# A two-layer mixture-of-experts block: the two-sided decayed sum as a scan of a scan, with its clamps on GpSimd, and another order in layer 0's routed tiles

## Chip, cores and metric

One core of one Trainium2 chip runs the whole program. The metric is the device time of one execution in microseconds (us); a time stands for the median of several runs. A profile is one execution seen by the hardware profiler: engines are PE (TensorE, matrix products), PEld (its weight loads), DVE (VectorE), ACT (ScalarE), POOL (GpSimd) and SP (SyncE, which issues DMAs).

## The reference, cut to what matters

There are two layers. Each has a "cond" step that mixes a side input k (4 x 512 x 512) along time, and a feed-forward step with routed experts plus a shared expert. All in float32. With T = 512 time steps and C = 512 channels, for each batch b and channel c:

```
tf    = sigmoid(sum(time_emb))
decay = exp(-exp(w)) * (0.5 + 0.5*tf)            # one number per (b, c), below 1
ek    = exp(min(k, 30));  ekv = ek * v           # v is k here
a[t]  = a[t-1]*decay + e[t]                      # scan forward  -> nf (of ekv), df (of ek)
a[t]  = a[t+1]*decay + e[t]                      # scan backward -> nb, db
euk   = exp(min(u + k, 30))
num   = nf + nb - ekv + euk*v;  den = df + db - ek + euk
out   = sigmoid(x) * num / max(den, 1e-8) * (0.8 + 0.2*tf)
```

So each of num and den is a two-sided sum, over all s, of decay^|t-s| e[s], plus one more term. Layer 0's feed-forward is: RMS norm, softmax over 8 experts, the top 2, SiLU-gated experts of width 256, and a shared expert of width 256. Layer 1's: softmax over 32 experts, the top 6, experts of width 352, a shared expert of width 704. Each layer adds its result to x.

## The kernel before

**Layer 0's loop of units.** A unit is one batch b (of 4) and one block c of 128 channels (of 4): 16 units, channels on the partitions and 512 time steps along the free axis. The order on ACT, PE and DVE is the program's own (a manual schedule); POOL and SP are ordered by the tile framework's planner. Iteration n of the loop does, in this order: `sums(n-1)`, `front(n+1)`, `front_exps(n+1)`, `turn(n+3)`, then routing and shared-expert pieces of the batch before, `mid(n)`, and `back(n-1)`.

- `turn` transposes k's rows on PE into `kA`. The rows of one batch lie in the tile `kr`, of which there is one; `load_k(b+1)` is asked for on SP once the last unit of batch b has been turned, together with `load_x(b+1)`.
- `front` (L401 to L409) does the two clamps on DVE (`ek` L406, `euk` L408), `front_exps` the exponentials on ACT (L414).
- `mid` multiplies with k on DVE (`ekv` L425, `eukv` L426) and calls `scans` (L258): for ek and for ekv one scan forward over 512 steps (L263) and one backward over 511 steps that leaves the own element out (L264), each into a tile of its own. Four scans a unit.
- `sums` adds the three parts on PE into PSUM, with an identity as the weight: `den` = df + dx + euk, `num` = -(nf + nx + eukv) times the batch's factor: six matrix products a unit (L436 to L438). ACT makes a reciprocal from den (`r`, L440 to L442).
- `back` (L449 to L452) makes num/den and multiplies it onto the sigmoids in `zT`.

Between units lie layer 0's router (`route_*`), whose slots are written one indirect DMA per (tile, choice) from POOL into `table0` (`fill_table`, L353), and the shared expert for some tiles (`share_*`). At the start POOL also writes the blank tables (L248 to L250) and 16 blocks of zeros to the DRAM tensor `xb` (L254).

**Layer 0's routed tiles.** `routed(0, ...)` runs expert after expert, in tiles of 128 rows, the first unconditionally, the others under nested `tc.If(n > s*P)` (L892). `slot_tile` puts on PE: gate products (L835), the transposes of the hidden rows of the tile before (`turn_hidden`, L799), up products (L839), the transposes of the next tile's rows (`turn_rows` into `pza`, L785), and the down products of the tile before (`put_out` into `pout`, L813). On ACT: SiLU (`sgt`, L842), the copy of the hidden rows of the tile before (`hT`, L804), the scaled up result (`upt`, L845), four scaled copies of the transposed rows (`zgT`, L789), the copy of `pout` to `ob` (L815) and of `last` (L862). On POOL: the product `hrow` (L846), the gather of the tile after the next (L772, an indirect DMA), and the scatter-add of the tile before (L818). In layer 0 the gate's and the up's results share one PSUM bank (`pgu`), and `pout` has one bank: three banks (`late`) are held for the shared expert's last three tiles.

Beside the routed tiles DVE does layer 1's two-sided sums (`wkv1`: 16 units, L915 to L925, into `kA`). They are needed when layer 1 begins. Then come the last three shared tiles, layer 1's input with its router (L965 to L986), layer 1's shared expert with the router's slots (L1060 to L1072), and layer 1's routed tiles.

Of the kernel before, what the change touches and what calls it, by code (L numbers as in the profile page):

```python
# [25 lines left out]
DEN_MIN = 1e-8  # L26
EXP_LN = "natural_log_exp_and_others"
# [3 lines left out]
def adaln_ffn_kernel(  # L31
# [90 lines left out]
    def load_k(b):  # L122
        kr = wk.tile([P, TB, D], F32, tag="kr", name=f"kr{b}", bufs=1)
        nc.sync.dma_start(kr, kf[b * S : (b + 1) * S, :].rearrange("(i p) c -> p i c", p=P))
        return kr
# [54 lines left out]
    kr = wk.tile([P, TB, D], F32, tag="kr", name="kr0", bufs=1)  # L180
    for i in range(TB):
        nc.scalar.dma_start(kr[:, i, :], kf[i * P : (i + 1) * P, :])
    load_x(0)
    gaten = acc[:E1, NT - 3, :]
# [9 lines left out]
            engines={mybir.EngineType.Activation, mybir.EngineType.PE, mybir.EngineType.DVE}  # L194
# [20 lines left out]
    for l in range(2):  # L215
        ew = const.tile([P, NC], F32, name=f"ew{l}")
        nc.scalar.activation(ew, wch[l], AF.Exp)
        dw = const.tile([P, NC], F32, name=f"dw{l}")
        nc.scalar.activation(dw, ew, AF.Exp, scale=-1.0)
        dec = const.tile([P, NC, B], F32, name=f"dec{l}")  # L220
        nc.vector.tensor_tensor(
            dec, dw.unsqueeze(2).to_broadcast([P, NC, B]), half.unsqueeze(1).to_broadcast([P, NC, B]), ALU.mult
        )
        decay.append(dec)
# [20 lines left out]
    for tb, width in ((table0, 3), (table1, 2)):  # L245
        blank = wk.tile([P, NCOL * width], F32, name=f"blank{width}", tag="lgT", bufs=1)
        bv = blank.rearrange("p (c w) -> p c w", w=width)
        nc.gpsimd.memset(bv, 0.0)  # L248
        nc.gpsimd.memset(bv[:, :, 0], EMPTY)
        nc.gpsimd.dma_start(tb.rearrange("(p c) w -> p (c w)", p=P), blank)  # L250
    zero = wk.tile([P, D], F32, name="zero", tag="zr", bufs=TB)
    nc.gpsimd.memset(zero, 0.0)
    for t in range(NT):
        nc.gpsimd.dma_start(xb[t * P : (t + 1) * P, :], zero)  # L254


    L = S - 1

    def scans(l, b, c, ek, ekv, df, dx, nf, nx):

        dec = decay[l][:, c, b : b + 1]
        for v, f, r in ((ek, df, dx), (ekv, nf, nx)):
            nc.vector.tensor_tensor_scan(f, dec.to_broadcast([P, S]), v, 0.0, ALU.mult, ALU.add)  # L263
            nc.vector.tensor_tensor_scan(  # L264
                r[:, L - 1 :: -1],
                v[:, L:0:-1],
                dec.to_broadcast([P, L]),
                0.0,
                ALU.add,
                ALU.mult,  # L270
            )

# [113 lines left out]
    def turn(n):  # L386

        nonlocal kr
        if n >= NU:
            return  # L390
        b, c = units[n]
        pk = bank("tr", f"pk{n}")
        for i in range(TB):
            nc.tensor.transpose(pk[:, i * P : (i + 1) * P], kr[:, i, c * P : (c + 1) * P], ident)
        nc.scalar.copy(kA[:, c, b * S : (b + 1) * S], pk)
        if c == NC - 1 and b + 1 < NB:
            kr = load_k(b + 1)
            load_x(b + 1)

    def front(n):  # L400
# [4 lines left out]
        ek = wk.tile([P, S], F32, tag="ek", name=f"ek{n}", bufs=2)  # L405
        nc.vector.tensor_scalar(ek, kT, 30.0, None, ALU.min)  # L406
        euk = wk.tile([P, S], F32, tag="euk", name=f"euk{n}", bufs=3)
        nc.vector.tensor_scalar(euk, kT, uch[0][:, c : c + 1], 30.0, ALU.add, ALU.min)  # L408
        fronts[n] = ek, euk  # L409

    def front_exps(n):
        if n < NU:
            for v in fronts[n]:
                nc.scalar.activation(v, v, AF.Exp)  # L414

    def mid(n):
        b, c = units[n]
        kT = kA[:, c, b * S : (b + 1) * S]
        ek, euk = fronts.pop(n)

        def tmp(tag, bufs=2):
            return wk.tile([P, S], F32, tag=tag, name=f"{tag}{n}", bufs=bufs)

        ekv, eukv = tmp("ekv", 1), tmp("eukv")
        nc.vector.tensor_tensor(ekv, ek, kT, ALU.mult)  # L425
        nc.vector.tensor_tensor(eukv, euk, kT, ALU.mult)  # L426
        df, dx, nf, nx = tmp("df"), tmp("dx"), tmp("nf"), tmp("nx")
        scans(0, b, c, ek, ekv, df, dx, nf, nx)
        mids[n] = (df, dx, euk), (nf, nx, eukv)

    def sums(n):
# [3 lines left out]
        for p, m, (f, r, o) in zip((den, num), (ident, nfac[:, b, :]), mids.pop(n)):  # L435
            nc.tensor.matmul(p, m, f, start=True, stop=False)  # L436
            nc.tensor.matmul(p[:, :L], m, r[:, :L], start=False, stop=False)
# [124 lines left out]
    def route_slots(b):  # L562
# [4 lines left out]
        through(fill_table(table0, sloti, pay, TB, 2, "table0" if b == NB - 1 else None))  # L567
# [53 lines left out]
    def exps1_upto(m):  # L621
        nonlocal done
        while done < m:
# [3 lines left out]
            nc.scalar.activation(ek, kT, AF.Exp)  # L627
# [13 lines left out]
    for n in range(NU + 1):  # L641
        b, c = divmod(n, NC)
        if n:
            sums(n - 1)
        front(n + 1)
# [29 lines left out]
        if c == 3 and b >= 1:  # L675
            route_slots(b - 1)
        if c == 2 and b >= 1:
# [34 lines left out]
    route_slots(NB - 1)  # L712
    counts0 = const.tile([P, E0], I32, name="counts0")
# [26 lines left out]
    def routed(l, pool, px, E, NS, chunks, zd, tab, put_at, counts, outs, first_weights, load, then=None, extra={}):  # L740
# [3 lines left out]
        if l == 0:  # L744
            pgu = px.tile([P, 2 * F], F32, name="pgu0")
            pg, pu = pgu[:, :F], pgu[:, F:]
        else:
            pg = px.tile([P, F], F32, name="pgate1")
            pu = px.tile([P, F], F32, name="pup1")
        pout = [px.tile([P, D], F32, name=f"pout{l}{h}") for h in range(1 + l)]  # L750
# [77 lines left out]
        def slot_tile(e, s, wts, due):  # L828

            gv, uv, _ = wts  # L830
            zt = turned(e, s)
            if due is not None and l == 1:
# [19 lines left out]
            gather(e, s + 2)  # L852
# [46 lines left out]
        return ahead, pza, phT  # L899

    latep = ExitStack()
    late_ps = latep.enter_context(tc.tile_pool(name="late", bufs=1, space=PSUM))
    late_out = [late_ps.tile([P, D], F32, name=f"late{t}") for t in range(LATE, NT)]
    with tc.tile_pool(name="r0", bufs=1) as rp, tc.tile_pool(name="px0", bufs=1, space=PSUM) as px:
# [5 lines left out]
        def wkv1(n):  # L910
# [3 lines left out]
            ekv, df, dx, nf, nx = [rp.tile([P, S], F32, tag=f"v{i}", name=f"v{i}_{n}") for i in range(5)]  # L914
            nc.vector.tensor_scalar(ek, ek, E30, None, ALU.min)  # L915
            nc.vector.tensor_tensor(ekv, ek, kT, ALU.mult)
            scans(1, b, c, ek, ekv, df, dx, nf, nx)
            nc.vector.tensor_tensor(df[:, :L], df[:, :L], dx[:, :L], ALU.add)
            nc.vector.tensor_tensor(nf[:, :L], nf[:, :L], nx[:, :L], ALU.add)
            nc.vector.scalar_tensor_tensor(df, euk, E30, df, ALU.min, ALU.add)  # L920
            nc.vector.scalar_tensor_tensor(ekv, euk, E30, kT, ALU.min, ALU.mult)
            nc.vector.tensor_tensor(nf, nf, ekv, ALU.add)
            nc.vector.tensor_scalar(df, df, DEN_MIN, None, ALU.max)
            nc.vector.reciprocal(df, df)
            nc.vector.scalar_tensor_tensor(kT, nf, fac[:, b : b + 1], df, ALU.mult, ALU.mult)  # L925
# [13 lines left out]
        with tc.manual_schedule(engines={mybir.EngineType.Pool, mybir.EngineType.PE, mybir.EngineType.Activation}):  # L939
            (wnext,), pza, phT = routed(  # L940
# [5 lines left out]
            for t in range(LATE, NT):  # L946
# [3 lines left out]
                if t > LATE:  # L950
                    share_turn(t - 1, phT)
                    share_down(t - 1, po=late_out[t - 1 - LATE])
            share_turn(NT - 1, phT)
            share_down(NT - 1, po=late_out[NT - 1 - LATE])
# [38 lines left out]
    latep.close()  # L993
# [120 lines left out]
```

## Time and profile before

| | |
|---|---|
| median of 3 runs | 1601.48 us (1598.72 to 1601.71) |
| the profiled execution: its time, its span | 1601.9 us, 1600.1 us |
| PE busy | 1458.0 us (91%) |
| DVE busy | 678.1 us (42%) |
| POOL busy | 593.0 us (37%) |
| ACT busy | 399.9 us (25%) |

The stages, read from the timeline: start to 44 us the first loads and the first three units; to about 205 us the rest of layer 0's loop; to 262 us the last router batch and shared tiles; to 557 us layer 0's routed tiles; to 626 us the late shared tiles and layer 1's input; the rest is layer 1. A number in front of a timeline row is the start in us from the span's beginning, the next the duration; what stands in brackets is the idle time of that engine ahead of it and what ended it. "issue" is time in which the engine waited for nothing that the profile shows.

### The profile page before, as it was taken

What the parts mean: (1) busy time and instruction counts of PE and PEld (TensorE: products, weight loads), DVE (VectorE), ACT (ScalarE), POOL (GpSimd) and SP (SyncE); (2) the same over time, 40 slices, a digit from 0 to 9 for tenths busy, and PEclk for the clock granted to TensorE, in tenths of its full rate; (3) what the DMA queues carried; (4) which work ended last, traced back from release to release, by engine and by line L of the source; (5) the groups of instructions that cost most, each with busy time, mean ns of one, the idle gap of its engine ahead of it and who ended that gap; (6) DMA issues with size and microseconds to landing.
All of it is one profiled execution on the core that took longest, in us unless ns stands there. A gap on an engine that the chain in (4) does not pass through costs nothing. (4 is left out here: it accounts for less than half of the span.)

```text
span 1600.1 us, 16354 instructions
## 1 busy us (share of the span) xinstructions
PE 1458.0 (91%) x5097; PEld 860.8 (54%) x5097; DVE 678.1 (42%) x1192; ACT 399.9 (25%) x966; POOL 593.0 (37%) x576
## 2 busy tenths in 40 slices
PE   4878988979788788999999999999999999999997
PEld 2445555656555466444444565555555555655654
DVE  6897956999960035261111222222222222222221
ACT  4755534454333324000000111111111111111110
POOL 3020133767654300016663333344333443433332
PEclk8999999999989879999999999999999999999999
DMA  9210114444545364001113655565645585565542
GB/s 351 80 33 34 40 47 163 73 100 77 111 109 125 86 223 153 1 1 43 39 46 109 181 150 130 145 191 153 164 109 136 128 266 119 130 187 131 122 99 40
DMA packets 117177, 184.95 MB, mean 116 GB/s; under 512 B 19928, under 2 KB 65004, under 8 KB 117016
## 3 DMA queue, kind: packets, MB, share of 16 engines
q1 hardware_dynamic: 80120, 122.14, 22.6%
q0 software_dynamic: 36336, 60.04, 19.8%
q8 instruction: 66, 1.08, 0.3%
q10 hardware_dynamic: 576, 1.05, 0.2%
q14 instruction: 79, 0.65, 0.1%
HBM read 152.07 MB, written 52.64 MB: 128 GB/s over the span
## 5 line engine op out<-in xcount | busy, mean ns | idle before, releaser
L813 PE MATMUL pout<-w,hT 128*128 128x512 f32 (+1 forms) x432 | 206.9, 612 | 10.6 <-ACT hT L804 9.3
L818 POOL DMA_INDIRECT out_dram<-ob,put x52 | 82.6, 1589 | 282.7 <-DVE ob L817 142.2
L772 POOL DMA_INDIRECT acc<-z1d,put x119 | 123.3, 1036 | 136.7 <-PE pza L785 58.9
L353 POOL DMA_INDIRECT table<-pay,r1sloti x96 | 93.3, 972 | 195.1 <-DVE hid L1063 168.6
L851 DVE SCALAR_TENSOR_TENSOR hrow<-pup,tab,sgt 128x352 f32<-128x352 f32 x84 | 49.1, 584 | 257.6 <-issue 131.2
L835 PE MATMUL pgate<-w,zgT 128*128 128x352 f32 x416 | 133.2, 463 | 0.1
L839 PE MATMUL pup<-w,zgT 128*128 128x352 f32 x416 | 131.5, 459 | 0.0
L817 DVE COPY ob<-pout 128x512 f32<-128x512 f32 x84 | 58.1, 692 | 172.7 <-PE pout L813 166.8
L813 PEld LDWEIGHTS pout<-w,hT 128*128 128x128 f32 (+1 forms) x432 | 77.8, 194 | 83.8 <-issue 55.7
L785 PE MATMUL pza<-ident,acc 128*128 128x128 f32 x584 | 88.8, 277 | 21.3 <-DMA acc<-z0d,put 18.1
L785 PEld LDWEIGHTS pza<-ident,acc 128*128 128x128 f32 x584 | 71.7, 142 | 65.3 <-issue 27.5
L353 POOL DMA_INDIRECT table<-r0pay,r0sloti x32 | 36.0, 1125 | 182.9 <-DVE r0sloti L343 137.4
L839 PEld LDWEIGHTS pup<-w,zgT 128*128 128x128 f32 x416 | 79.0, 190 | 44.0
L835 PEld LDWEIGHTS pgate<-w,zgT 128*128 128x128 f32 x416 | 75.8, 192 | 34.0 <-issue 1.2
L808 ACT COPY hT<-phT 96x128 f32<-96x128 f32 x84 | 22.0, 262 | 285.3 <-DVE hT L806 285.3
L1060 PE MATMUL g<-zT,w 128*128 128x512 f32 (+1 forms) x192 | 89.3, 609 | 4.2 <-DVE lg L991 4.2
L795 ACT COPY zgT<-pza 128x256 f32<-128x256 f32 x103 | 38.3, 373 | 210.3 <-DVE zgT L794 158.7
L813 PE MATMUL pout<-zT,hT 128*128 128x512 f32 (+1 forms) x192 | 87.8, 593 | 0.0
L1060 PE MATMUL u<-zT,w 128*128 128x512 f32 (+1 forms) x192 | 86.3, 592 | 0.0
L1069 PE MATMUL o<-w,hid 128*128 128x512 f32 (+1 forms) x192 | 83.8, 592 | 0.0
L835 PE MATMUL pgate<-zT,zgT 128*128 128x352 f32 x256 | 81.0, 459 | 0.0
L839 PE MATMUL pup<-zT,zgT 128*128 128x352 f32 x256 | 81.0, 459 | 0.0
(279 smaller groups left out, 2346.9 us busy)
## 6 DMA issues: line engine op xcount, KB each, us to landing
w<-in_L_ffn_w_dram SPq DMA_DIRECT2D x44, 704.0 KB, 5.9
zT<-in_L_ffn_w_dram SPq DMA_DIRECT2D x20, 704.0 KB, 5.0
w<-in_L_ffn_w_dram SPq DMA_DIRECT2D x22, 512.0 KB
zT<-in_L_ffn_w_dram SPq DMA_DIRECT2D x10, 512.0 KB
w<-in_L_ffn_w_dram SPq DMA_DIRECT2D x22, 192.0 KB, 8.9
xb<-zero POOLq DMA_DIRECT2D x16, 256.0 KB, 7.8
acc<-in_x_dram SPq DMA_DIRECT2D x4, 1024.0 KB, 15.2
z0d<-zr SPq DMA_DIRECT2D x16, 256.0 KB, 2.0
```

The lines of the kernel that those rows point to most:

```text
L353: ins = nc.gpsimd.indirect_dma_start(out=table, out_offset=bass.IndirectOffsetOnAxis(ap=sloti[:, t, j : j + 1], axis=0), in_=pay[:, t, j, ...
L772: nc.gpsimd.indirect_dma_start(out=rows(e, s), out_offset=None, in_=zd, in_offset=bass.IndirectOffsetOnAxis(ap=put_at[:, e * NS + s : e * ...
L785: nc.tensor.transpose(pza[which][:, c * P : (c + 1) * P], rows(e, s)[:, c * P : (c + 1) * P], ident)
L795: nc.scalar.copy(dst[:, h:, :], pza[which][:, h * P :].rearrange("p (c t) -> p c t", c=h))
L813: nc.tensor.matmul(po, hT[:m, j, :], dv[:m, j, :], start=(j == 0), stop=(j == nf - 1))
L817: nc.vector.tensor_copy(row, po)
L818: nc.gpsimd.indirect_dma_start(out=outs[n % len(outs)], out_offset=bass.IndirectOffsetOnAxis(ap=at, axis=0), in_=row, in_offset=None, boun ...
L835: nc.tensor.matmul(pg, zt[:, c, :], gv[:, c, :], start=(c == 0), stop=(c == NC - 1))
L839: nc.tensor.matmul(pu, zt[:, c, :], uv[:, c, :], start=(c == 0), stop=(c == NC - 1))
L851: nc.vector.scalar_tensor_tensor(hrow, pu, tab[:, col, 1:2], sgt, ALU.mult, ALU.mult)
L1060: nc.tensor.matmul(p[:m], wv[:, c, f : f + m], zT[:, c, cols], start=(c == 0), stop=(c == NC - 1))
L1069: nc.tensor.matmul(po, hid[:m, j, i * P : (i + 1) * P], dv[:m, j, :], start=(j == 0), stop=(j == len(FCH) - 1))
```

## The change

Four things, in one step.

1. **A scan of a scan.** Each e is scaled by 1 - decay^2 (as a bias ln(1 - decay^2) in the exponential, so without another instruction), scanned backward in place, its first element is multiplied by 1/(1 - decay^2), and it is scanned forward in place. That gives the two-sided sum in one tile, so that `sums` needs four matrix products a unit instead of six, and `wkv1` two additions less. The decays are held below 1, and `lom`, `inv` and `cap` are made once at the start.
2. **GpSimd.** `front`'s two clamps and `mid`'s `eukv` go from DVE to POOL. POOL's order in layer 0's loop is now the program's own. One block of zeros is written to `xb` per iteration, the blank tables at iteration 2, and the slots of each batch 2 or 3 at a time in several iterations (all in one group without order among them).
3. **k's rows** have two buffers, and the second batch is asked for at the start, right after the first batch of x.
4. **Layer 0's routed tiles:** gate and up have a bank each and `pout` two; the late shared tiles are copied by ACT to rows of `acc` in SBUF instead of staying in PSUM; and the gather of tile s + 2 is put on POOL ahead of `hrow` instead of after it.

```diff
-        kr = wk.tile([P, TB, D], F32, tag="kr", name=f"kr{b}", bufs=1)
+        kr = wk.tile([P, TB, D], F32, tag="kr", name=f"kr{b}")
...
     load_x(0)
+    krs.append(load_k(1))
...
-            engines={mybir.EngineType.Activation, mybir.EngineType.PE, mybir.EngineType.DVE}
+            engines={
+                mybir.EngineType.Activation, mybir.EngineType.PE, mybir.EngineType.DVE, mybir.EngineType.Pool
+            }
...
-        decay.append(dec)
+        nc.vector.tensor_scalar(dec, dec, NEAR_1, None, ALU.min)
+        om = const.tile([P, NC, B], F32, name=f"om{l}")
+        nc.vector.tensor_scalar(om, dec, -1.0, 1.0, ALU.mult, ALU.add)
+        nc.vector.scalar_tensor_tensor(om, dec, 1.0, om, ALU.add, ALU.mult)
+        lom = const.tile([P, NC, B], F32, name=f"lom{l}")
+        nc.scalar.activation(lom, om, AF.Ln)
+        inv = const.tile([P, NC, B], F32, name=f"inv{l}")
+        nc.vector.reciprocal(inv, om)
+        cap = const.tile([P, NC, B], F32, name=f"cap{l}")
+        nc.vector.tensor_scalar(cap, om, E30, None, ALU.mult)
+        decay.append((dec, cap, lom, inv))
...
-        for v, f, r in ((ek, df, dx), (ekv, nf, nx)):
-            nc.vector.tensor_tensor_scan(f, dec.to_broadcast([P, S]), v, 0.0, ALU.mult, ALU.add)
+        dec, _, _, inv = (m[:, c, b : b + 1] for m in decay[l])
+        for h in range(2):
             nc.vector.tensor_tensor_scan(
-                r[:, L - 1 :: -1],
-                v[:, L:0:-1],
-                dec.to_broadcast([P, L]),
-                0.0,
-                ALU.add,
-                ALU.mult,
+                v[:, h, ::-1], dec.to_broadcast([P, S]), v[:, h, ::-1], 0.0, ALU.mult, ALU.add
             )
+        nc.vector.tensor_scalar(v[:, :, 0], v[:, :, 0], inv, None, ALU.mult)
+        for h in range(2):
+            nc.vector.tensor_tensor_scan(v[:, h, :], dec.to_broadcast([P, S]), v[:, h, :], 0.0, ALU.mult, ALU.add)
...
-        nc.vector.tensor_scalar(ek, kT, 30.0, None, ALU.min)
+        v = wk.tile([P, 2, S], F32, tag="v2", name=f"v2_{n}", bufs=3)
+        nc.gpsimd.tensor_scalar(v[:, 0, :], kT, 30.0, None, ALU.min)
         euk = wk.tile([P, S], F32, tag="euk", name=f"euk{n}", bufs=3)
-        nc.vector.tensor_scalar(euk, kT, uch[0][:, c : c + 1], 30.0, ALU.add, ALU.min)
+        nc.gpsimd.tensor_scalar(euk, kT, uch[0][:, c : c + 1], 30.0, ALU.add, ALU.min)
...
-        nc.vector.tensor_tensor(ekv, ek, kT, ALU.mult)
-        nc.vector.tensor_tensor(eukv, euk, kT, ALU.mult)
+        nc.gpsimd.tensor_tensor(eukv, euk, kT, ALU.mult)
+        nc.vector.tensor_tensor(v[:, 1, :], v[:, 0, :], kT, ALU.mult)
...
-        for p, m, (f, r, o) in zip((den, num), (ident, nfac[:, b, :]), mids.pop(n)):
-            nc.tensor.matmul(p, m, f, start=True, stop=False)
-            nc.tensor.matmul(p[:, :L], m, r[:, :L], start=False, stop=False)
+        for p, m, (d, o) in zip((den, num), (ident, nfac[:, b, :]), mids.pop(n)):
+            nc.tensor.matmul(p, m, d, start=True, stop=False)
             nc.tensor.matmul(p, m, o, start=False, stop=True)
...
         if n:
             sums(n - 1)
+            nc.gpsimd.dma_start(xb[(n - 1) * P : n * P, :], zero)
+        if n == 2:
+            blank_tables()
...
             route_slots(b - 1)
+            write_slots(b - 1, 3)
+        if c < 2 and b >= 2:
+            write_slots(b - 2, 3 - c if b < NB else 5)
...
-        if l == 0:
-            pgu = px.tile([P, 2 * F], F32, name="pgu0")
-            pg, pu = pgu[:, :F], pgu[:, F:]
-        else:
-            pg = px.tile([P, F], F32, name="pgate1")
-            pu = px.tile([P, F], F32, name="pup1")
-        pout = [px.tile([P, D], F32, name=f"pout{l}{h}") for h in range(1 + l)]
+        pg = px.tile([P, D], F32, name=f"pgate{l}")[:, :F]
+        pu = px.tile([P, D], F32, name=f"pup{l}")[:, :F]
+        pout = [px.tile([P, D], F32, name=f"pout{l}{h}") for h in range(2)]
...
             zt = turned(e, s)
+            if l == 0:
+                gather(e, s + 2)
...
-            gather(e, s + 2)
+            if l == 1:
+                gather(e, s + 2)
...
-    late_out = [late_ps.tile([P, D], F32, name=f"late{t}") for t in range(LATE, NT)]
+    late_out = [acc[:, NT // 2 + h, :] for h in range(NT - LATE)]
...
-                    share_down(t - 1, po=late_out[t - 1 - LATE])
+                    share_down(t - 1, po=pout[t % 2])
+                    nc.scalar.copy(late_out[t - 1 - LATE], pout[t % 2])
```

## The prediction

> **What bounds the kernel now.** I read the page's busy slices first, then a table of busy time by stage, then who waited for whom in the two stages that the change edits, then single rows of the timeline. By stage (columns: window, its length, PE, PEld, DVE, ACT, POOL busy with counts, granted clock, DMA share, GB/s):
>
> ```profile
> 44.00:205.00 161.00, 141.90 (x481) 75.94 (x479) 145.10 (x316) 95.71 (x179) 19.98 (x16) 0.96 0.11 40
> 205.00:262.00 57.00, 51.15 (x195) 34.16 (x196) 24.95 (x82) 25.95 (x50) 18.02 (x19) 0.94 0.19 65
> 262.00:468.00 206.00, 169.35 (x686) 118.11 (x685) 205.99 (x213) 87.66 (x265) 135.33 (x87) 0.94 0.48 109
> 468.00:557.00 89.00, 70.04 (x256) 47.60 (x257) 0.00 (x1) 32.81 (x104) 36.92 (x33) 0.86 0.46 106
> 760.00:1600.00 840.00, 810.92 (x2786) 466.21 (x2784) 194.93 (x383) 105.91 (x282) 332.80 (x349) 0.99 0.51 132
> ```
>
> Layer 1 (from 626 us) is PE's and is not edited; nothing there can move by more than its start. In layer 0's loop (44 to 205 us) DVE is busy 145 of 161 us and PE 142: DVE is the nearer bound, PE close behind. In the routed tiles (262 to 557 us) DVE is full up to 468 us with layer 1's sums, but nobody waits for them before 580 us; PE is busy 239 of 295 us, so 56 us are waits of PE.
>
> Who DVE waited for between 12 and 206 us, and one unit of DVE without a wait:
>
> ```profile
> DVE t L449 <- ACT r L442: 7.7, 2, 6.9
> DVE r0sm L291 <- ACT r0pr L288: 3.8, 1, 3.8
> DVE v L501 <- ACT sq L471: 3.7, 2, 2.1
> DVE lg L516 <- PE plt L491: 1.7, 1, 1.7
> ```
>
> ```profile
> 169.03 0.42 DVE L406 TENSOR_SCALAR ek<-kA 128x512 f32<-128x512 f32 x1
> 169.36 0.48 DVE L408 TENSOR_SCALAR euk<-kA,chan 128x512 f32<-128x512 f32 x1
> 169.75 0.68 DVE L425 TENSOR_TENSOR ekv<-ek,kA 128x512 f32<-128x512 f32 x1
> 170.36 0.69 DVE L426 TENSOR_TENSOR eukv<-euk,kA 128x512 f32<-128x512 f32 x1
> 170.96 1.22 DVE L263 TENSOR_TENSOR_SCAN df<-dec,ek 128x512 f32<-128x512 f32 x1
> ```
>
> The next unit starts at 178.34: a unit costs DVE 9.3 us (front 0.72, the two products 1.21, four scans at 1.12, `back` 2.85), and a dozen small router operations come on top. The 6.9 us wait is k's second batch: PE stands for 8.0 us until 35.69 us on the DMA of `kr`, asked for at 22.34 us behind the weights and the 4 MB of zeros to `xb`.
>
> Who PE waited for between 262 and 562 us, the larger groups:
>
> ```profile
> PE pza L785 <- DMA acc<-z0d,put: 18.1, 14, 3.3
> PE pout L813 <- ACT hT L804: 9.8, 17, 2.7
> PE pgu L835 <- PEq L892: 8.1, 3, 3.7
> PE pgu L835 <- ACTq L892: 7.7, 3, 4.1
> PE phT L799 <- POOLq L892: 5.6, 1, 5.6
> ```
>
> The last three are the walk past the untaken tiles of an expert, which the change leaves. The first is a gather that lands late; the second is a copy on ACT that stands behind SiLU, and SiLU waits for the up product although it reads the gate's, since both lie in one bank.
>
> **POOL beside DVE.** The rows that price the move to GpSimd:
>
> ```profile
> 326.87 1.20 DVE L263 TENSOR_TENSOR_SCAN v<-dec,acc 128x512 f32<-128x512 f32 x1
> 327.02 1.56 POOL L846 TENSOR_TENSOR hrow<-upt,sgt 128x256 f32<-128x256 f32 x1 [1.95 <-ACT upt L845]
> 327.99 1.69 DVE L263 TENSOR_TENSOR_SCAN v<-dec,v 128x512 f32<-128x512 f32 x1
> 485.11 0.72 POOL L846 TENSOR_TENSOR hrow<-upt,sgt 128x256 f32<-128x256 f32 x1 [2.55 <-ACT upt L845]
> ```
>
> With DVE idle `hrow` takes 0.72 us. Issued during a scan it ends 0.51 us after the scan's end, and the scan that follows takes 1.69 instead of 1.20 us. So here the two engines take turns: POOL's 256-element product costs DVE 0.49 us. Issued at 279.64 ahead of five DVE operations in a row, four of them with two inputs, it took 3.45 us, and ended 0.68 us after the reciprocal (3.35 us, no slower for it) began.
>
> The Trainium skill (GPSIMD Engine Reference, section 8, Key points) says the same in general: GpSimd shares its SBUF interfaces with VectorE and contends with DVE instructions that have two SBUF inputs; its section 4.1 advises against elementwise work on GpSimd beside such an engine. That speaks against this part of the change. Were that rule the whole story, all of POOL's time would come on top of DVE's, as in the third case below, and the sum would be slower; the rows say that it doesn't against the reciprocal.
>
> **The loop, part by part (before: 12 to 205 us).**
> - Removed from DVE: two clamps (0.33 + 0.40 us by the spacing of the starts) and `eukv` (0.60): 1.33 us a unit.
> - Added to DVE: one 128x2 operation, 0.2 us by the 128x4 rows (0.16 us, 0.20 apart), and three waits for a result of its own (product to scan, scan to small operation, small operation to scan). `back`'s operations, which wait so, start 0.72 us apart against 0.60 for others of that length: 0.12 us each, 0.36. The scans stay four; I take 1.12 us for in-place ones too. Net -0.77 us, over 15 units -12 us. The first unit counts with the start.
> - POOL against DVE: `eukv` of 512 elements at twice `hrow`'s 0.49 us is 0.98. A one-input clamp of 512 has no row on POOL; below it lies the 128x512 memset (0.52 us, hence 0.5), above it the two-input rate (0.98). I take 0.5, since a clamp moves one input and one output where the product moves two and one. Sum 2.0 us a unit. Some of that falls in DVE's operations that read PSUM (2 x 0.69 us), in its waits for its own results or in waits for others; I take a quarter as hidden: 1.5 x 16 = +24 us. Bounds: 0 (all hidden) and 2.94 x 16 = +47 us (all at the two-input rate, nothing hidden).
> - Behind the waiting POOL instruction: the clamps of unit n + 1 and `eukv` of n queue behind the zeros (0.55 us each), the blank tables (iteration 2; the second waits some 5 us for the first one's DMA) and up to three slot writes (1.0 to 1.9 us each) that wait for DVE's `r0sloti`. ACT's exponentials of n + 1 wait for the clamps, and what ACT has behind them. But they are needed only when DVE has done `back` and a `mid` more, some 8 us; the writes take about 5. I cost this at nothing; uncovered it would be about 3 us in each of four iterations.
> - k's second batch asked for at about 4 us instead of 22: the wait of 6.9 us goes. What is late next is nothing near: x's second batch is due at 45 us. The 4 MB of zeros leave the start too.
> - PE: two matrix products less a unit, 0.86 us each at full clock: 27 us off PE, so DVE's waits that go back to PE's backlog (3.8 + 3.7 + 1.7 + the other 0.8 us) should halve: -5 us.
> - Four clamps of `wkv1` (0.4 us each) that DVE did inside the loop must now wait for a tile that is free only after it: -1.6 us.
> - Start: two chains of five small operations on DVE and two logarithms on ACT ahead of k's copies: 0.2 us apart, some of it beside the clock of the loads: +1.5 us.
>
> Sum: -12 + 24 - 6.9 - 5 - 1.6 + 1.5 = 0 us. The loop moves in its content and not in its length. The tail (205 to 262 us) is PE's and stays; POOL's last slot writes and the first gather (issued at 250.0) are done some 7 us before PE is ready (261.9), which covers them.
>
> **The routed tiles.**
> - SiLU no longer waits for the up product (1.9 us earlier), so `hT` is ready before `pza` ends: 9.8 us of waits go but for the 2.67 us at 360.70, where ACT is busy with layer 1's exponentials: -7 us.
> - The gather ahead of `hrow`: of 18.1 us, the first two waits (3.28 + 0.63) belong to gathers that are not moved. The others, 14.1 us, are gathers asked for behind an `hrow` that itself waited up to 6 us: -14 us.
> - In return `hrow` stands behind a gather of 1.0 to 1.8 us. PE wants it about 3 us after `upt`; it takes 0.7 to 3 us. I charge +3 us for the tiles where both are long (before: 3.2 us of waits for `hrow`, three times).
> - After stalls of 2 us and more PE ran at half speed (3.62 us for four products at 469.17 that take 1.98 otherwise). Two or three such stalls go: -2 us.
> - The second `pout` bank and 18 us less of `wkv1` meet no wait; the three ACT copies of the late tiles (0.6 us each) lie beside the DMA of `other`, which lands 3 us after the last product: nothing, or +0.7 us if that cover goes.
>
> Sum: -20 us, between -6 (only the `hT` waits) and -26.
>
> **Total.** 0 - 20 on the profiled execution's 1601.9 us is 1582; that execution is 0.4 us above the median of 1601.48, hence **1581.5 us**.
>
> **The rivals.**
> 1. The forecast: loop level, routed tiles 20 us shorter. Chance 0.55.
> 2. POOL hides better than I think: its work falls in `back` and in waits, the contention is near 0 to 6 us, the loop gains about 20: 1560 us. For it: the reciprocal's row, and `hrow` at 361.17 (0.86 us) beside it. Against: scans are 4.5 of DVE's 8.5 us a unit. Chance 0.2.
> 3. Slower, by one mechanism: POOL's three operations a unit in layer 0's loop take DVE's turn. If clamps go at the two-input rate and nothing hides, +47 instead of +24: 1605 us. It decides from 1.5 + 20/16 = 2.75 us of DVE's time lost per unit. For it: the scan of 1.69 us. Chance 0.15.
> 4. The routed tiles don't shorten, since the gathers' landing (3.4 to 4.2 us after issue) and `hrow` behind them take the waits over, and the loop is level: 1600 us. Against: the large waits stand behind idle POOL time. Chance 0.10.
>
> **How the numbers follow.** The range 1560 to 1603 reaches from case 2 to just below case 3 and takes in the loop's -24 to +20 at the forecast's routed gain. A measurement of this kernel can tell 0.2%, 3.2 us. Faster by more: case 1, case 2 and a part of case 4, 0.79; within: the middle of cases 3 and 4, 0.07; slower: 0.14.
>
> **What would show it.** In the profile after: scans in the loop with a mean above 1.4 us (contention) or at 1.2 (case 2); POOL clamps near 0.7 to 1.0 us when alone; no wait of DVE on `r` near 43 us; PE's waits on the gather and on `hT` in the routed tiles under 8 us together; that stage about 275 us long, its start still near 262. I am wrong if the start of the routed tiles moves by over 20 us, or the stage itself by under 8.

## The result, and the profile after

The changed kernel takes 1651.72 us (median of 4 runs, 1647.96 to 1667.59) against 1601.60 us of the kernel before: a ratio of 1.0336, 95% interval 1.0268 to 1.0404. The forecast was 1581.5 us, within 1560 to 1603: the direction and the size are both wrong. The profiled execution takes 1650.74 us, its span 1648.6 us.

The page's busy tenths in 40 slices of 41 us:

```profile
PE   5768788979777306899999999999999999999997
DVE  6987856994000996534111222222222222222221
```

The 3 and the 0 in PE's line (slices 14 and 15, 536 to 618 us) are new. In the same slices DVE has 9s, after three slices of 0. So PE does next to nothing while DVE is full, and just before that DVE did nothing while PE was full. The table by stage gives the lengths (columns as before: window, length, busy time of PE, PEld, DVE, ACT, POOL with counts, granted clock, DMA share, GB/s):

```profile
44.00:205.00 161.00, 121.42 (x408) 68.19 (x408) 138.38 (x270) 94.91 (x174) 97.88 (x66) 0.86 0.15 55
205.00:267.00 62.00, 56.13 (x204) 35.75 (x202) 28.86 (x89) 26.85 (x51) 18.97 (x20) 0.93 0.18 63
267.00:389.00 122.00, 108.42 (x462) 80.03 (x463) 117.35 (x119) 64.65 (x181) 74.10 (x56) 0.94 0.53 118
389.00:539.00 150.00, 120.74 (x502) 86.59 (x501) 0.00 (x0) 62.39 (x192) 71.74 (x64) 0.93 0.50 117
539.00:632.00 93.00, 13.21 (x48) 8.08 (x46) 87.83 (x95) 3.61 (x8) 0.00 (x0) 0.60 0.15 49
```

The timeline of DVE in the changed kernel, where it stops and where it goes on:

```profile
387.55 0.75 DVE L944 SCALAR_TENSOR_TENSOR kA<-v,fac 128x512 f32<-128x512 f32 x1
388.41 0.49 DVE L935 TENSOR_SCALAR v<-zT,cap 128x512 f32<-128x512 f32 x1
539.03 0.48 DVE L606 SCALAR_TENSOR_TENSOR shr<-pza,rs,ssg 128x256 f32<-128x256 f32 x1 [150.13 <-ACT ssg L600]
539.43 0.68 DVE L936 TENSOR_TENSOR v<-v,kA 128x512 f32<-128x512 f32 x1
...
626.46 0.75 DVE L944 SCALAR_TENSOR_TENSOR kA<-v,fac 128x512 f32<-128x512 f32 x1
```

At 388.41 DVE does the first operation of unit 9 of layer 1's sums (`wkv1`). The next instruction in its queue is `shr`, the first of the last three shared tiles' products. It needs ACT's `ssg`, which needs PE's products of that tile, and these stand behind the last routed tile. So DVE stands for 150.13 us, with the rest of unit 9 and units 10 to 15 behind the waiting product: 87 us of work, done from 539.43 to 627.2 us. Layer 1's input needs the late rows and then the sums, in DVE's order. The loads of `other`, the second summand of those rows, leave SP only at 627.41 us, right behind the last sum (at 577.38 us in the kernel before). So PE waits:

```profile
PE pt L994 <- DVE acc L991: 78.8, 2, 78.1
```

In the kernel before this wait was 4.7 us. Its DVE waited too, 94.54 us for the same product (L591 there), but only the last operation of unit 15 (0.74 us) stood behind it. DVE's rows and PE's wait there:

```profile
562.54 0.48 DVE L591 SCALAR_TENSOR_TENSOR shr<-pza,rs,ssg 128x256 f32<-128x256 f32 x1 [94.54 <-ACT ssg L585]
562.95 0.74 DVE L925 SCALAR_TENSOR_TENSOR kA<-v,fac,v 128x512 f32<-128x512 f32 x1
```

```profile
PE pt L973 <- DVE acc L970: 5.3, 2, 4.7
```

The order of the two queues is in the program as built: in the routed stage the program fixes the order of POOL, PE and ACT, and the planner places DVE's instructions. The change made it place the product nearly seven units earlier.

Up to that point the changed kernel leads. The first late product begins at 539.03 us against 562.54 before, 23.5 us earlier. Its PE waits in the routed stage (262 to 545 us):

```profile
PE pza L803 <- DMA acc<-z0d,put: 8.9, 5, 2.6
...
PE pout L831 <- ACT hT L822: 3.9, 2, 3.4
...
PE phT L817 <- POOL hrow L866: 2.1, 2, 1.3
```

Against 18.1, 9.8 and 3.2 us before. In layer 0's loop POOL's three operations, by line (columns: count, then busy us and mean ns, then idle time before and its cause):

```profile
L420 POOL TENSOR_SCALAR euk<-kA,chan 128x512 f32<-128x512 f32 x16 | 36.1, 2259 | 1.5
L418 POOL TENSOR_SCALAR v<-kA 128x512 f32<-128x512 f32 x16 | 29.5, 1844 | 19.3 <-ACT kA L406 10.7 <-PE num L445 5.3 <-ACT rsg L512 2.2
L435 POOL TENSOR_TENSOR eukv<-euk,kA 128x512 f32<-128x512 f32 x16 | 26.1, 1632 | 8.2 <-ACT euk L428 7.0
```

and what DVE waited for up to 210 us, the largest group in the loop and the one that the change was to remove:

```profile
DVE v L509 <- ACT sq L479: 9.1, 1, 9.1
...
DVE t L457 <- ACT r L450: 3.3, 2, 2.2
```

The wait of 6.9 us for k's second batch is gone; a wait of 9.1 us elsewhere is new.

### The profile page after: what moved, and what is told of

Same layout as the page of the kernel before. It is cut to its first block, busy times and chain, and to the rows that moved or that the text cites. A ratio compares the mean times of both kernels' runs of the same rounds, so it can differ in the third digit from the quotient of the medians.

```text
span 1648.6 us, 16340 instructions
## 1 busy us (share of the span) xinstructions
PE 1424.6 (86%) x5033; PEld 848.8 (51%) x5033; DVE 675.1 (41%) x1154; ACT 410.0 (25%) x971; POOL 658.1 (40%) x624
## 5 line engine op out<-in xcount | busy, mean ns | idle before, releaser
L855 PE MATMUL pgate<-w,zgT 128*128 128x352 f32 (+1 forms) x656 | 194.6, 441 | 16.4 <-PEq L913 12.2
L831 PE MATMUL pout<-w,hT 128*128 128x512 f32 (+1 forms) x432 | 202.6, 601 | 4.7 <-ACT hT L822 3.9
L859 PE MATMUL pup<-w,zgT 128*128 128x352 f32 (+1 forms) x656 | 189.3, 432 | 0.0
L855 PEld LDWEIGHTS pgate<-w,zgT 128*128 128x128 f32 x656 | 123.5, 195 | 71.5 <-issue 24.4
L859 PEld LDWEIGHTS pup<-w,zgT 128*128 128x128 f32 x656 | 123.5, 192 | 49.0
L790 POOL DMA_INDIRECT acc<-z0d,put x51 | 58.6, 1149 | 71.2 <-issue 15.5
L994 PE MATMUL pt<-ident,acc 128*128 128x128 f32 x64 | 13.1, 352 | 79.6 <-DVE acc L991 78.8
```

The source lines that it names most:

```text
L790: nc.gpsimd.indirect_dma_start(out=rows(e, s), out_offset=None, in_=zd, in_offset=bass.IndirectOffsetOnAxis(ap=put_at[:, e * NS + s : e * ...
L831: nc.tensor.matmul(po, hT[:m, j, :], dv[:m, j, :], start=(j == 0), stop=(j == nf - 1))
L855: nc.tensor.matmul(pg, zt[:, c, :], gv[:, c, :], start=(c == 0), stop=(c == NC - 1))
L859: nc.tensor.matmul(pu, zt[:, c, :], uv[:, c, :], start=(c == 0), stop=(c == NC - 1))
```

## The experiments

**The table** puts side by side what one profiled execution of each shows: start of the routed tiles (first transposes into `pza`), first late product on DVE, first transposes of layer 1's input, first product of layer 1's shared expert (all us from the span's start), and the median of the runs.

| | routed | late product | input | layer 1 | median |
|---|---|---|---|---|---|
| before | 261.9 | 562.5 | 582.0 | 625.3 | 1601.6 |
| changed | 267.1 | 539.0 | 632.3 | 676.2 | 1651.7 |
| 1 | 264.1 | 538.5 | 558.4 | 613.6 | 1582.0 |
| 2 | 261.8 | 559.4 | 578.8 | 622.0 | 1600.6 |
| 3 | 261.7 | 558.8 | 652.8 | 689.8 | 1665.2 |
| 4 | 255.6 | 527.3 | 547.3 | 602.4 | 1575.0 |
| 5 | 260.6 | 531.5 | 551.7 | 596.8 | 1569.8 |
| 6 | 268.0 | 542.8 | 562.7 | 612.3 | 1576.0 |
| 7 | 257.5 | 535.9 | 555.8 | 605.2 | 1580.0 |
| 8 | 255.2 | 551.3 | 571.2 | 620.6 | 1592.2 |
| 9 | 263.4 | 535.2 | 555.0 | 598.9 | 1580.1 |
| 10 | 261.9 | 536.6 | 556.5 | 611.6 | 1582.8 |
| 11 | 267.4 | 541.3 | 561.2 | 605.9 | 1581.1 |
| 12 | 262.1 | 533.3 | 553.0 | 597.6 | 1567.4 |

How far a number of one execution can be trusted is read from rows with the same work: the same loop starts the routed tiles at 264.1, 267.1 and 267.4 us (1, changed, 11) and at 255.6, 257.5 and 255.2 us (4, 7, 8), so a start is good to some 3 us.

### Where the 50 us went: DVE's queue (1, 2, 3, 11)

**1. The changed kernel with DVE in program order.**

```diff
-        with tc.manual_schedule(engines={mybir.EngineType.Pool, mybir.EngineType.PE, mybir.EngineType.Activation}):
+        with tc.manual_schedule(
+            engines={mybir.EngineType.Pool, mybir.EngineType.PE, mybir.EngineType.Activation, mybir.EngineType.DVE}
+        ):
```

> The changed kernel with one addition: VectorE's order in layer 0's routed stage is also the program's, so the six units of layer 1's sums that it held back (10 to 15) and the rest of unit 9 stand ahead of the late shared tiles' products. Theory A (the loss is VectorE standing 150 us behind the first late product, with 85 us of sums queued behind it): PE's wait of 78.1 us for layer 1's first sum of rows falls to the 4.7 us of the kernel before, so 1650.7 - 73.5 = 1577 us; part of that may go again (up to 9 us), since VectorE is then busy beside GpSimd's products until about 475 us: 1577 to 1586. Rival B (the loss is GpSimd's work beside VectorE in layer 0's loop, or another cost of the change): the loop is not touched, and the time stays above 1640.

Measured: 1582.01 us, ratio to before 0.9887 (0.9860 to 0.9914). PE's wait for the first late rows is back at the size of before:

```profile
PE pt L996 <- DVE acc L993: 5.6, 2, 5.0
```

Theory A holds, rival B falls. Layer 0's loop is that of the changed kernel, and 70 us are gone.

**2. The kernel before with the same line.**

> The kernel before with the same addition. There only the last operation of unit 15 (0.74 us) stood behind the first late product, so theory A expects no change: 1598 to 1604 us. If the addition itself brings the gain of the experiment beside it (rival), it is faster here too, by 10 us or more.

Measured: 1600.55 us, ratio 0.9992 (0.9973 to 1.0012). The fixed order brings nothing by itself.

**3. The kernel before, units 10 to 15 put behind the late products.**

```diff
         def wkv1_rest():
             exps1_upto(NU)
             nc.scalar.preload_act_table_set("silu_and_others")
-            for n in range(10, NU):
-                wkv1(n)
...
                 share_hid(t)
+                if t == NT - 1:
+                    for n in range(10, NU):
+                        wkv1(n)
```

(with the order of experiment 2)

> The kernel before, VectorE in program order, with units 10 to 15 of layer 1's sums put behind the third late product instead of ahead of the first; nothing else of the change. Theory A: the third late product ends at about 573 us, then six units of 12.9 us follow, 77 us, with PE idle; layer 1's input starts at about 651 instead of 582 us, so 1670 us (1660 to 1678), a loss larger than that of the change. Rival B: the place of these units costs little, since VectorE idles 95 us before: 1600 to 1610 us.

Measured: 1665.15 us, ratio 1.0405 (1.0381 to 1.0428). PE's waits around layer 1's input:

```profile
PE pt L975 <- DVE acc L972: 80.0, 2, 79.3
```

The place alone makes the loss, without any other part of the change. The forecast of 1670 is 5 us high: the input stage behind it took 37.0 us instead of 43.3 (below, on the clock).

**11. The changed kernel with two buffers for `v2` in `wkv1`**, DVE again in the planner's order.

```diff
-            v = rp.tile([P, 2, S], F32, tag="v2", name=f"v2_{n}", bufs=1)
+            v = rp.tile([P, 2, S], F32, tag="v2", name=f"v2_{n}", bufs=2)
```

> The changed kernel with two buffers instead of one for the tile v2 of layer 1's sums (wkv1); VectorE's order in the routed stage is the planner's again. In the program as built this puts the first late product ahead of the last unit's forward scans only, instead of ahead of the rest of unit 9 and six more units. Theory (one buffer made the units a chain that the planner expected to last longer than the routed stage, and the product's place in VectorE's queue is the whole loss): some 9 us of sums stay behind the first late product and are done before the last of the late shared tiles and their DMA, 19 us later, so PE's wait for layer 1's first rows is near 5 us again: 1575 to 1588 us, as in the first experiment. Rival (the loss hangs on VectorE's fixed order, or the waits for own results in the new sums cost more than the place): above 1600 us.

Measured: 1581.13 us, ratio 0.9876 (0.9839 to 0.9913). DVE's timeline:

```profile
541.34 0.48 DVE L606 SCALAR_TENSOR_TENSOR shr<-pza,rs,ssg 128x256 f32<-128x256 f32 x1 [84.89 <-ACT ssg L600]
541.74 2.33 DVE L283 TENSOR_TENSOR_SCAN v<-dec,v 128x512 f32<-128x512 f32 x2
...
550.11 0.75 DVE L944 SCALAR_TENSOR_TENSOR kA<-v,fac 128x512 f32<-128x512 f32 x1
...
559.64 0.69 DVE L989 TENSOR_TENSOR acc<-acc,other 128x512 f32<-128x512 f32 x1 [8.10 <-DMA other<-xb]
```

The product still stands ahead of some sums, but of 9 us of them, and these end 9 us before the next DMA lands. So one digit, the number of buffers of a tile on DVE, decides here where the planner puts an instruction of another stage. Four kernels ran with DVE in the planner's order there: in the kernel before, with the old scans, one operation stands behind the product, in the changed kernel nearly seven units, and with two buffers (this one and experiment 12) a part of the last unit. How the planner weighs this no run shows.

### What GpSimd costs in layer 0's loop (4, 5, 6, 9)

**4. Experiment 1 with the clamps and `eukv` back on DVE.**

```diff
-        nc.gpsimd.tensor_scalar(v[:, 0, :], kT, 30.0, None, ALU.min)
+        nc.vector.tensor_scalar(v[:, 0, :], kT, 30.0, None, ALU.min)
...
-        nc.gpsimd.tensor_scalar(euk, kT, uch[0][:, c : c + 1], 30.0, ALU.add, ALU.min)
+        nc.vector.tensor_scalar(euk, kT, uch[0][:, c : c + 1], 30.0, ALU.add, ALU.min)
...
-        nc.gpsimd.tensor_tensor(eukv, euk, kT, ALU.mult)
+        nc.vector.tensor_tensor(eukv, euk, kT, ALU.mult)
```

> The first experiment's kernel with the two clamps and the product eukv of layer 0's loop back on VectorE. Theory (the loop's 5.3 us of loss come from GpSimd taking VectorE's turn, about 29 us by the forecast's own terms, against the 1.33 us x 16 = 21 us that the three operations cost on VectorE): routed tiles start about 8 us earlier, near 259 us, and the time is 5 to 10 us below the first experiment's. Rival (GpSimd hides most, and the 5.3 us are something else): 12 to 21 us above it.

Measured: 1574.95 us, ratio 0.9824 (0.9788 to 0.9861); the routed tiles start at 255.6 us, 8.5 us earlier than in experiment 1. As expected in size. But the two loops run level up to the ninth `back` (118.33 and 118.36 us): until there what POOL takes from DVE only cancels the operations that it took over. The one unit behind it takes 23.3 us in experiment 1 and 14.1 us here, and the rest of the loop 2.4 us more; the tail gives 3 us back. So the 8.5 us are no steady contention. Waits in experiment 1 between 100 and 135 us:

```profile
POOL table L365 <- DVE r0sloti L355: 17.2, 1, 17.2
DVE v L509 <- ACT sq L479: 8.2, 1, 8.2
...
PE pk L405 <- ACT shT L615: 7.1, 1, 7.1
ACT v L427 <- POOL v L418: 6.5, 2, 6.1
```

and POOL's timeline there:

```profile
110.51 1.35 POOL L365 DMA_INDIRECT table<-r0pay,r0sloti  x1 [0.15 <-issue]
112.17 1.12 POOL L365 DMA_INDIRECT table<-r0pay,r0sloti  x1 [0.30 <-issue]
113.59 1.48 POOL L365 DMA_INDIRECT table<-r0pay,r0sloti  x1 [0.30 <-issue]
115.05 0.62 POOL L660 DMA_DIRECT2D xb<-zero  x1
115.75 2.47 POOL L418 TENSOR_SCALAR v<-kA 128x512 f32<-128x512 f32 x1
118.31 2.00 POOL L420 TENSOR_SCALAR euk<-kA,chan 128x512 f32<-128x512 f32 x1
```

POOL waits for DVE's slot numbers until 100 us, then works without a gap to 130.7. The clamps come late behind three slot writes and a block of zeros; ACT stands 6.1 us on them with `shT` behind; PE stands 7.1 us on `shT` with the router's transposes behind; DVE stands 8.2 us on those. Four engines, one queue.

**5 and 6. Experiment 4 with only `eukv`, and with only the clamps, on GpSimd** (one and two of the three edits of experiment 4 left out).

> The fourth experiment's kernel (VectorE in program order, GpSimd free of layer 0's loop; routed tiles from 255.6 us, 1575 us) with only the product eukv on GpSimd. Off VectorE: 0.60 us x 16 = 9.6 us. Theory (the forecast's price of the product holds, 0.98 us with a quarter hidden, 12 us in all, and the two clamps are what was sized too low): routed tiles from about 258 us. Rival (the product alone carries the contention, 30 us by the difference of the first and fourth experiments: 8.5 us net plus 21 us of operations moved off): from about 276 us, later than the first experiment's 264.

> The same base with only the two clamps on GpSimd. Off VectorE: 0.73 us x 16 = 11.7 us. Theory (the clamps, 1.9 and 2.2 us each beside VectorE instead of the 0.5 us that the forecast took, carry the larger part of the 30 us of contention, 18 us): routed tiles from about 262 us. Rival (clamps cost 0.5 us of VectorE's time each with a quarter hidden, 12 us in all): from about 256 us.

Measured: 5 starts the routed tiles at 260.6 us (1569.80 us, ratio 0.9797, 0.9765 to 0.9830), 6 at 268.0 us (1575.96 us, 0.9819, 0.9782 to 0.9856). With the moved operations taken off, the product costs 260.6 - (255.6 - 9.6) = 14.6 us and the clamps 268.0 - (255.6 - 11.7) = 24.1 us. The order is that of the theory. The product's sum is within a start's 3 us of the theory's 12, the clamps' is larger than its 18. The two don't add up to the 30 us of experiment 1, and in 6 the unit behind the ninth `back` again takes 21.5 us, 7 us of the clamps' sum lie in that unit. The medians of 4 and 5 don't follow the starts; the intervals overlap, and the input stage of 4 ran longer at half clock (below).

**9. Experiment 1 with all slot writes behind the loop.**

```diff
-            write_slots(b - 1, 3)
-        if c < 2 and b >= 2:
-            write_slots(b - 2, 3 - c if b < NB else 5)
...
-    write_slots(NB - 1, TB * 2)
+    for b in range(NB):
+        write_slots(b, TB * 2)
```

(with four buffers for the slot numbers and their payload)

> The first experiment's kernel (VectorE in program order, all three operations on GpSimd) with the slot writes of all batches put on GpSimd behind the loop of units instead of 2 or 3 in an iteration; nothing else. Theory (what GpSimd's work costs the loop is its queue: three slot writes and a block of zeros, 110.5 to 115.7 us, stand ahead of the clamps, ACT waits 6.1 us for them, PE 7.1 us for ACT's shT behind that, VectorE 8.2 us, so that the unit begun at 118.3 us takes 23.3 us against 14.1 without GpSimd): that unit takes 14 to 16 us, and the routed tiles start at 254 to 257 us instead of 264, provided that the 32 writes, some 40 us, fit in the 60 us behind the loop. Rival (the cost is the clamps' own 1.9 to 2.2 us and VectorE's slower scans, wherever the writes stand): the routed tiles start at 262 to 265 us, or later where the writes hold up the first gathers.

Measured: 1580.06 us, ratio 0.9880 (0.9855 to 0.9905). The unit takes 14.9 us (119.71 to 134.64 us), and the loop's last `back` begins at 204.95 us, against 216.00 in experiment 1 and 204.48 in experiment 4. So in the loop the queue was it, some 11 us. But the routed tiles start at 263.4 us, which is the rival's range and level with experiment 1: the tail gives it back. Waits from 205 to 270 us in this kernel:

```profile
DVE v L509 <- ACT sq L479: 16.6, 1, 16.6
...
PE plt L499 <- ACT lgT L493: 9.4, 1, 9.4
```

While the first 24 writes run (188.7 to 220.2 us) and just behind them, ACT's `sq` stands 8.5, 2.9 and 2.2 us; in experiment 4 it stands 3.9 us once. For the 8.5 us the profile names PE's products `pl`, which `sq` does not read, for the other two no instruction of the program; so what holds it stays open. The theory was right on the loop and wrong on the total.

### What the routed tiles gain, and from what (7, 8, 10)

**7. Experiment 4 with the gather behind `hrow` again**, as in the kernel before.

> The fourth experiment's kernel with the gather of layer 0's tile s + 2 put on GpSimd behind hrow again. Theory (the forecast's term: 14 us of waits for gathers saved, 3 us of waits for hrow paid): PE's waits for the gather in the routed stage go from 6.4 to about 17 to 20 us, those for hrow from 4.3 to about 3; the stage from its first transposes to the first late product, 271.7 us, becomes about 11 us longer. Rival (with gate and up in two banks and pout in two, PE no longer meets the late gather): the stage stays within 3 us.

Measured: 1580.02 us, ratio 0.9846 (0.9813 to 0.9880). The stage takes 278.4 us against 271.7: 6.7 us longer. PE's waits in it:

```profile
PE pza L803 <- DMA acc<-z0d,put: 16.6, 11, 3.8
...
PE pout L831 <- ACT hT L822: 3.8, 2, 3.3
```

The waits for gathers grow by 10.2 us, those for `hrow` shrink from 4.3 to 1.4 us. Right in kind, 6.7 instead of 11. The same stage takes 270.9 to 274.8 us in experiments 1, 4, 5, 6, 9, 11 and 12, so this size is good to some 4 us.

**8. Experiment 4 with layer 0's gate and up in one bank.**

```diff
-        pg = px.tile([P, D], F32, name=f"pgate{l}")[:, :F]
-        pu = px.tile([P, D], F32, name=f"pup{l}")[:, :F]
+        if l == 0:
+            pgu = px.tile([P, 2 * F], F32, name="pgu0")
+            pg, pu = pgu[:, :F], pgu[:, F:]
...
```

> The fourth experiment's kernel with layer 0's gate and up results in one PSUM bank again (pout keeps its two banks). Theory (the forecast's term: SiLU waits for the up product again, 1.9 us): PE's waits for hT go from 4.2 to about 10 us, over some 17 tiles, and the stage of 271.7 us becomes 5 to 9 us longer. Rival (the second pout bank carries that gain, or it lies beside waits for gathers): the stage stays within 2 us.

Measured: 1592.21 us, ratio 0.9936 (0.9915 to 0.9958). The stage takes 296.1 us, 24.4 us longer than with two banks, and not 5 to 9:

```profile
PE pout L835 <- ACT hT L826: 20.0, 27, 7.7
PE pgu L859 <- ACTq L917: 9.3, 3, 4.0
```

**10. The kernel before with part 4 alone**, DVE in program order: the banks, the copies of the late tiles and the gather ahead of `hrow` from the change's diff, nothing of the scans, of GpSimd in the loop, of k's buffers.

> The kernel before with only the fourth part of the change (banks of gate, up and pout, late tiles copied, gather ahead of hrow) and VectorE in program order. Theory (that part alone carries the gain of some 26 us in the routed stage, and the scans, GpSimd and k's buffers together are worth 6 us less or more): routed tiles from 261.9 us, 271 to 275 us to the first late product, 1573 to 1578 us. Rival (the stage's gain needs the rest of the change, for instance GpSimd's or VectorE's lighter work on layer 1's sums beside the routed tiles): the stage keeps 285 us or more, 1587 us or more.

Measured: 1582.80 us, ratio 0.9851 (0.9809 to 0.9893). The stage takes 274.7 us, as the theory has it: part 4 alone brings 26 us there. The median lies 5 us above the theory's range; its six runs go from 1565.7 to 1588.0 us, and the profiled one (1587.95) has the long half clock of the input stage. Experiment 1, with all four parts, takes 1582.01 us: the other three parts together bring nothing that the times show.

### A version that beats both

**12. The changed kernel with two buffers for `v2` in `wkv1` and the clamps on DVE**, `eukv` left on GpSimd.

> The same kernel with the two clamps of layer 0's loop back on VectorE, the product eukv left on GpSimd. Theory (from the fifth experiment, whose loop this is): routed tiles from about 260.6 us, stage 271 to 275 us, 1568 to 1578 us, faster than the kernel before by about 2% and than the changed kernel by 5%. Rival: as with the experiment beside it, above 1600 us.

Measured: 1567.44 us (1566.58 to 1571.26, 5 runs), ratio 0.9783 (0.9761 to 0.9805) to the kernel before. Three lines away from the changed kernel, it is 84 us, 5.1%, below the changed kernel's median of 1651.72.

## Why the prediction was wrong, step by step

**The step that failed** is the sentence on layer 1's sums: "DVE is full up to 468 us with layer 1's sums, but nobody waits for them before 580 us", and after it that less of `wkv1` would "meet no wait". The wait was put at nothing and measured 78.1 us, against 4.7 in the kernel before. The sentence took DVE's order as given. The order in that stage is the planner's, and the change edits what the planner plans. The table that the prediction shows had the sign in it: from 468 to 557 us DVE has 0.00 us busy with one instruction, and what follows is an operation of unit 15 behind the late product. That was an instruction waiting at the head of DVE's queue, with one operation behind it. What stands behind it in the changed program was not asked; the order of a program is there once it is built (the expectation of experiment 11 reads it so), and it had nearly seven units there. Nor did the "18 us less of `wkv1`" come: its units, one after the other, take 13.4 us each in experiment 1 and 12.9 in the kernel before. Experiments 1, 2, 3 and 11 show that this place in the queue is the whole loss: without it the same change takes 1582.01 us, and the forecast was 1581.5. That they agree so closely is partly luck: in experiment 1 the loop is 2.2 us longer than before, the routed stage 26.3 shorter, and in the profiled execution the half clock of the input stage adds 11.8.

**The loop: 0 forecast, +5.3 us measured** (start of the routed tiles 267.1 against 261.9; +2.2 in experiment 1).
- Contention of POOL and DVE, forecast 1.5 us a unit. From first to last `back`, 15 units, experiment 9 takes 172.1 us and experiment 4, without POOL's work, 174.1; the three operations off DVE are 15 x 1.33 = 20 us, so POOL took 18 us back, 1.2 us a unit (and experiment 9's first `back` is 2.5 us later). The term holds in its sum, and rival 3 (2.75 us a unit) falls, though its sign came true. Of the 91.7 us that POOL's three operations are busy in the changed kernel, most is hidden. So the contention that the Trainium skill states (GPSIMD Engine Reference, section 8, Key points) is there, with scans of 1.30 us against 1.21 in experiment 4, and far from the whole story. The clamps' part in it was sized from the wrong row: a clamp of one operation takes 1.5 us on POOL at the shortest and the one of two operations 2.0, not 0.7 to 1.0, and they make POOL's queue long.
- "I cost this at nothing" of POOL's queue: wrong, 8 to 9 us in one unit and some 11 us by the loop's end (experiments 4 and 9 against 1). The prediction named the queue, its members and the price if uncovered (3 us in each of four iterations). The cover of 8 us was computed without the clamps' own 4.5 us and the waits that ACT, PE and DVE pass on to each other.
- k's second batch: right. The second `back` follows the first after 9.8 us in experiment 4 instead of 16.2.
- The new scans without GpSimd: 9.8 us a unit in experiment 4 against 9.25; the forecast's terms give +0.56. Right.
- PE's two products less, forecast at -5 us of DVE's waits: near in experiment 4, where DVE's waits between 44 and 206 us, other than for k, are 3.3 us against 10.2 before. In the changed kernel POOL's queue puts its 9.1 us in their place. PE gave back less than 27 us: its busy time between 44 and 205 us falls by 20.5, while its granted clock there falls from 0.96 to 0.86.
- The start: +1.5 forecast; the first `back` begins 3.1 us later in experiment 4 and 4.4 in the changed kernel.

**The routed tiles: -20 forecast, -28.8 measured** (300.7 to 271.9 us). Some of that is spread: the old stage takes 297.5 and 297.0 us in experiments 2 and 3, the new one 270.9 to 274.8 us wherever it ran whole, so the gain is 22 to 30 us. That DVE stood idle in the changed kernel is no visible part of it: experiments 2 and 3, in which DVE stands idle for 86 and 170 us before the late product, differ by 0.5 us. The whole is near the forecast's outer bound of 26; the terms are not. The banks of gate and up, forecast at 7 us from the waits for `hT`, are worth 24.4 us when the rest is in place; the gather, forecast at 11 net, 6.7. What pout's second bank does alone no run shows. Two things were not to be seen in the list of waits. In experiment 8, with one bank and early gathers, PE stands 20.0 us on `hT` and 6.7 on gathers, in the kernel before 9.8 and 18.1, together nearly the same: the one wait had covered part of the other. And PE's busy time for the same 962 matrix instructions is 245.1 us in the kernel before, 240.8 in experiment 8 and 232.2 in experiment 4, at mean granted clocks of 0.91, 0.93 and 0.93; the forecast had put what PE's products lose behind stalls at 2 us. What shortens them by more, no run isolates.

**Late copies at nothing**: right; PE's wait for the late rows is 5.0 us in experiment 1 against 4.7.

**The test points.** Loop scans between the two marks (1.30 us mean); no wait on `r` near 43 us, as said; waits on gather and `hT` together 12.8 us, not under 8; clamps on POOL at 1.5 and 2.0 us, not 0.7 to 1.0; the stage near 275 and its start near 262, as said. "I am wrong if the start of the routed tiles moves by over 20 us, or the stage itself by under 8": neither happened. No test point lay between the stage's end and layer 1, where the 50 us were.

## What to carry to other kernels

An engine that a scheduler orders can get an instruction of a later stage into the middle of its queue; one that waited 95 us there cost nothing, one that waited 150 us cost 73, and the difference was what stood behind it. So look at what stands behind every long wait, in the built order of both kernels, before any sum of durations. One buffer more or less of a tile was enough to move it; where an order matters, write it out. A list of waits does not price a term by itself: another wait can cover part of it, and part can lie in an engine's busy time.

## What the runs showed of the hardware

**GpSimd's clamps are slower than its products.** On 128x512 a clamp takes 1.49 to 1.51 us, add and clamp 2.00 to 2.01, a product of two tiles 1.27 (the five shortest of the 16 each in the changed kernel). The Trainium skill (GPSIMD Engine Reference, section 4.1, Engine selection) says that one-input work is roughly at line rate there and two-input work about twice as slow as on VectorE; here DVE takes 0.42, 0.48 and 0.68 us for the three, so the one-input ones are the worse trade, by a factor of 3.6 and 4.2 against 1.9.

**TensorE at half clock while it is full.** In layer 1's input the granted clock is 0.50 for a time that differs from run to run. First the kernel before, then experiment 1, by windows of that stage:

```profile
590.00:597.00 7.00, 7.00 (x36) 7.00 (x36) 0.86 (x2) 1.34 (x3) 0.00 (x0) 0.50 0.25 98
...
604.00:611.00 7.00, 6.75 (x63) 6.44 (x62) 3.79 (x6) 4.32 (x8) 0.00 (x0) 1.00 0.86 296
```

```profile
566.00:574.00 8.00, 8.00 (x41) 8.00 (x40) 1.35 (x3) 1.76 (x3) 0.00 (x0) 0.50 0.32 104
...
590.00:598.00 8.00, 8.00 (x40) 8.00 (x40) 1.29 (x2) 2.03 (x5) 0.00 (x0) 0.50 0.36 125
```

In experiment 1 PE is busy without a gap from 566 to 598 us, the windows between these two included, and stays at half clock; a group of eight router products takes 1.75 us there and 0.98 at full clock. The Trainium skill (TensorE: Matmul & The Clock Gate, Part 1) has the full clock return after one busy window of about 3.4 us; these rows don't show that. The stage from its first transposes to layer 1's first product takes 43.3 us in the kernel before, 55.1 in experiments 1, 4 and 10, and 37.0 in experiment 3, where PE had stood for 79 us; but after a stand of 78 us in the changed kernel it takes 43.9. What decides it stays open. It makes some 12 us, in one pair 18, between profiled executions whose work in that stage is the same, and is why starts of stages, and not medians alone, were used above.
